# A graph layer on one core: bucket numbers moved to PSUM, and the node layer's own part worked out early

## The chip, the cores and the metric

The kernel runs on one core of a Trainium2 chip. A core has five engines with instruction queues of their own: TensorE (PE in the profile, with its weight loads as PEld), VectorE (DVE), ScalarE (ACT), GpSimd (POOL) and SyncE (SP). They share an on-chip memory, SBUF, of 128 partitions; matmuls write to a second memory, PSUM, of eight banks. Engines wait for each other by semaphores. DMAs move data between the chip's main memory and SBUF; they are issued from the queues of SP, ACT or POOL.

The metric is the device time of one execution in microseconds. Before the change three runs took 2500.06 (the median), 2503.01 and 2492.88 us.

## The reference

The kernel computes one layer of a graph network over 12500 nodes with 64 features and 212500 edges (`src`, `dst`, one weight each). The edges come ordered by `dst`. Cut to what matters:

```python
h = jnp.maximum(_layernorm(x, axis=-1), 0.0)
edge_in = jnp.concatenate([h[row], h[col], dist], axis=1)   # row = src, col = dst
e = silu(edge_in @ eW1 + eb1)
e = silu(e @ eW2 + eb2)
agg = segment_sum(e, row, num_segments=12500)
node_in = jnp.concatenate([h, agg], axis=1)
out = x + silu(node_in @ nW1 + nb1) @ nW2 + nb2
```

The hidden width is 128. `nW1` has 64 rows for the node's own `h` and 128 for the sums `agg`; the product with the first is "the part from a node's own rows".

## The kernel before, in words

The nodes are dealt into `NB` = 100 buckets of `L` = 125 nodes. An edge's bucket is that of its `src`. The kernel first writes the edges, in their given order, into bucket order in main memory (the array `q`), and then works bucket by bucket, so that the sums over `src` become matmuls.

**Tables.** `groups`, `normed` and `products` (L641 to L684) normalise the rows, turn them with PE (`turned`, tile `hr`, two buckets' features one above the other on 128 partitions), store the turned rows in main memory as `hd`, and multiply them by the two halves of `eW1`; the results are stored as the tables `ta` (for `src`) and `tb` (for `dst`). These are generators. They are strung together in `feed`, and each call of `next(feed)` issues one step of them, between other work.

**Sending.** The edges are sent in 208 blocks of 1024. `count(s)` (L344 to L410) ranks the edges of a block within their buckets on VectorE: `oh` (L352) compares the bucket numbers 1 to 100, from a constant row `nodes1` in SBUF, with each edge's bucket; `each` (L360) sums it over the block's 8 columns; PE adds `each` to `full` (L369, L387), a tile of PSUM that keeps the running counts of all buckets; `mine` (L402) multiplies `oh` by `full`, `rank` (L404) sums that, and `to` (L406) is the row number in `q`. `send(s)` (L412 to L467) makes the payload: `qp` (L427, PE) picks the `dst` table's rows, ACT copies it to `qs` (L437, L443), and POOL scatters 128 rows at a time with eight indirect DMAs (L450). There are 4 buffers of `to` and 8 of `qs`, so VectorE and ACT can be some blocks ahead of POOL.

**Buckets.** The rows of `q` are worked on in twelve levels of ranks, each as soon as the blocks that fill it are sent. A step takes four tiles of 128 edges: `lr` (L526) and `oneT` (L531) make the transposed one-hot of the node within the bucket, `pt` (L540, L546) adds the `src` table, ACT applies SiLU to `e` (L550), `p` (L578) is the second layer with its bias copied ahead (L572), SiLU again (L582), `one` (L559) is the one-hot, `seg` (L592) the sum by matmul, and `aggT` (L603) the running sum in SBUF. There are 450 steps.

**Node layer.** In the last level, whose 25 steps hold four buckets each, `nodes` (L239 to L260) follows each step. Two matmuls `z` multiply `aggT` by the lower part of `nW1` (L246), two more add the own rows' part from `hd` (L249), ACT applies SiLU (L251), four matmuls `o` multiply by `nW2` (L255), VectorE adds `x` (L258), and SP stores the result (L260). `nodes_in` (L230) loads `x` and `hd` when the level's rows are fetched, four steps ahead.

**Order.** The order on PE, VectorE, ACT and SP is written out by hand: the list `turn` (L610) names the parts of a step with their offsets in steps, and each `None` in it is a hook. At a hook some pieces of the sending are issued, so many that each level is sent in time (`marks`, L897), then up to two steps of `feed` while it lasts, then one piece of the oldest `nodes`. Each engine runs its queue strictly in that order:

```python
turn = [
    (s_pt, 1), (s_add, -2), (s_one_t, 2), None, (s_bias, 1), (s_p2, 0), (s_one, 0), None, (s_seg, -1), None, (s_lr, 3), None,
]
```

Of the kernel before, what the change touches and what calls it, by code (L numbers as in the profile page):

```python
# [28 lines left out]
F32 = mybir.dt.float32  # L29
# [3 lines left out]
AF = mybir.ActivationFunctionType  # L33
OP = mybir.AluOpType
# [4 lines left out]
P = 128  # L39
L = 125  # L40
# [8 lines left out]
TB = BLK // P  # L49
PAIR = 2 * BLK  # L50
BEYOND = 20
G = 4
# [9 lines left out]
FIRST = 4  # L62
# [11 lines left out]
def tile_gnn(ctx: ExitStack, tc: tile.TileContext, x, src, dst, ew, eW1, eb1, eW2, eb2, nW1, nb1, nW2, nb2, out):  # L74
    nc = tc.nc
    N, D = x.shape
# [3 lines left out]
    NB = N // L  # L80
    assert NB % G == 0 and NB <= P
    NP = -(-E // PAIR)
# [5 lines left out]
    dram = ctx.enter_context(tc.tile_pool(name="dram", bufs=1, space=DRAM))  # L88
# [28 lines left out]
    def rows16(dma, to, of):  # L117

        for part in (slice(0, 112), slice(112, L)):
            dma(to[part], of[part])  # L120
# [21 lines left out]
    nodes1 = const.tile([P, L], F32, name="nodes1")  # L142
    nc.vector.tensor_copy(nodes1, nodes_i)
    w1 = const.tile([P, 2, H], F32, name="w1")
    w1n = const.tile([P, H], F32, name="w1n")
# [61 lines left out]
            nc.scalar.copy(to.rearrange("l (i a) h -> l a i h", a=2)[:, a], abs_[a])  # L207

    hd = dram.tile([P, NB // 2, P], F32, name="hd")
    bkE = const.tile([P, 2 * TB, NP], F32, name="bkE")  # L210
    locE = const.tile([P, 2 * TB, NP], F32, name="locE")
    offE = const.tile([P, 2 * TB, NP], F32, name="offE")
# [17 lines left out]
    def nodes_in(B, sb):  # L230
        b = B * G
        xr = sb.tile([L, G, D], F32, name="xr")
        rows16(nc.sync.dma_start, xr, x_rows[:, b : b + G, :])
        nc.gpsimd.tensor_tensor(xr, xr, nb2b[:L, None, :].to_broadcast([L, G, D]), op=OP.add)
        hr = sb.tile([P, G // 2, P], F32, name="hrn")
        nc.sync.dma_start(hr, hd[:, b // 2 : b // 2 + G // 2, :])
        return xr, hr

    def nodes(B, xr, hr, ps, sb, tag):  # L239

        b = B * G

        zs = sb.tile([P, 2, G // 2, L], F32, name="zs")
        z = [ps.tile([P, G // 2, L], F32, name="z", tag=tag) for _ in range(2)]
        for a in range(2):
            nc.tensor.matmul(z[a], w1g, aggT[:, b + a : b + G : 2, :], start=True, stop=False)  # L246
        for a in range(2):
            half = slice(a * D, (a + 1) * D)
            nc.tensor.matmul(z[a], w1n[half, :], hr[half, :, :L], start=False, stop=True)  # L249
        for a in range(2):  # L250
            nc.scalar.activation(zs[:, a], z[a], AF.Silu, bias=nb1c)  # L251
        yield
        o = ps.tile([L, G, D], F32, name="o", tag=tag)
        for t in range(G):
            nc.tensor.matmul(o[:, t, :], zs[:, t % 2, t // 2, :], w2n, start=True, stop=True)  # L255
        yield
        os_ = sb.tile([L, G, D], F32, name="os")
        nc.vector.tensor_tensor(os_, o, xr, op=OP.add)  # L258
        yield
        rows16(nc.sync.dma_start, out_rows[:, b : b + G, :], os_)  # L260


    NQ = 4
# [5 lines left out]
    with ExitStack() as work:  # L269
# [5 lines left out]
                engines={mybir.EngineType.PE, mybir.EngineType.DVE, mybir.EngineType.Activation, mybir.EngineType.SP}  # L275
            )
        )
        full = sgp.tile([P, NB], F32, name="full")
        nc.tensor.matmul(full, before, identb[:, :NB], start=True, stop=True)
        nc.vector.memset(full, -1.0)  # L280
        mine = cnt.tile([P, TB, NB], F32, name="mine")
        sums = []
        blk, lists = {}, {}
# [60 lines left out]
        def count(s):  # L344

            if s < nblocks:
                bc, win, pick = blk[s]
                p, g = s // 2, s % 2
                whole = p > 0 and (2 * p + 2) * BLK <= E
                buckets = bkE[:, g * TB : (g + 1) * TB, p]  # L350
                oh = wk.tile([P, TB, NB], BF16, name="oh")
                nc.vector.tensor_tensor(  # L352
                    oh,
                    nodes1[:, None, :NB].to_broadcast([P, TB, NB]),
                    buckets[:, :, None].to_broadcast([P, TB, NB]),
                    op=OP.is_equal,
                )
                each = wk.tile([P, NB], BF16, name="each")
                with nc.allow_low_precision("whole numbers up to eight"):
                    nc.vector.tensor_reduce(each, oh.rearrange("p t b -> p b t"), AX.X, OP.add)  # L360
                if not whole:
                    nc.vector.tensor_scalar(pick, bc, same, plus, op0=OP.is_equal, op1=OP.add)
                elif g == 0:
                    nc.vector.tensor_scalar(lists[p][1], lists[p][0], same, plus, op0=OP.is_equal, op1=OP.add)
            yield
            if s < nblocks and (g == 0 or not whole):
                weights(s)
            if s > 0:
                nc.tensor.matmul(full, rest, sums.pop(), start=False, stop=True, skip_group_check=True)  # L369
            limits = [(SURE[w], OP.is_gt) for w in ready_at if s == ready_at[w]]  # L370
            closed = s > 0 and (s == nblocks or needed[s] != needed[s - 1])
            if closed:
                limits.append((SURE[needed[s - 1]], OP.is_lt))
            if s == nblocks:
                limits.append((ROWS, OP.is_gt))
            if limits:
                u = wk.tile([P, NB], F32, name="u")
                v = wk.tile([P, 1], F32, name="v")
            for limit, op in limits:
                nc.vector.tensor_scalar(u, full, float(G * limit - 1), None, op0=op)  # L380
                nc.vector.tensor_reduce(v, u, AX.X, OP.max)
                nc.vector.tensor_tensor(bad[:, 1:2], bad[:, 1:2], v, op=OP.add)
            if s == nblocks:
                return
            if closed and LEVELS[needed[s - 1]][2]:
                nc.vector.tensor_scalar(full, full, float(G * ENDS[needed[s - 1]] - 1), None, op0=OP.max)
            nc.tensor.matmul(full, before, each, start=False, stop=True, skip_group_check=True)  # L387
            sums.append(each)
            if g == 0:
                assert p in scaled  # L390
                both = bkE[:, :, p].rearrange("p (g t) -> p g t", g=2)
                wide = [P, 2, TB, TB]
                eq = wk.tile(wide, F32, name="eq")
                nc.vector.tensor_tensor(
                    eq, both[:, :, :, None].to_broadcast(wide), both[:, :, None, :].to_broadcast(wide), op=OP.is_equal
                )
                nc.vector.tensor_tensor(eq, eq, early[:, None].to_broadcast(wide), op=OP.mult)
                pre = wk.tile([P, 2 * TB], F32, name="pre")
                nc.vector.tensor_reduce(pre.rearrange("p (g t) -> p g t", g=2), eq, AX.X, OP.add)
                nc.vector.tensor_tensor(offE[:, :, p], offE[:, :, p], pre, op=OP.add)  # L400
            yield
            nc.vector.tensor_tensor(mine, oh, full[:, None, :].to_broadcast([P, TB, NB]), op=OP.mult)  # L402
            rank = wk.tile([P, TB], F32, name="rank")
            nc.vector.tensor_reduce(rank, mine, AX.X, OP.add)  # L404
            to = top.tile([P, TB], I32, name="to")
            nc.vector.scalar_tensor_tensor(  # L406
                to, rank, float(G * ROWS - 1), offE[:, g * TB : (g + 1) * TB, p], op0=OP.min, op1=OP.add
            )
            blk[s].append(to)
            yield  # L410
# [353 lines left out]
        def scale(p0, p1):  # L764

            v = bkE[:, :, p0:p1]

            q4 = lp.tile([P, 2 * TB, p1 - p0], F32, name="q4", tag=f"q4{p0}")
            nc.vector.tensor_scalar(q4, v, 0.5 - G / 2 - 1.0, 1.0 / G, op0=OP.add, op1=OP.mult)
            nc.vector.tensor_scalar(q4, q4, float(3 * 2**22), None, op0=OP.add)  # L770
            yield
            nc.vector.tensor_scalar(q4, q4, -float(3 * 2**22), None, op0=OP.add)
            nc.vector.scalar_tensor_tensor(offE[:, :, p0:p1], q4, float(ROWS * G - G), v, op0=OP.mult, op1=OP.add)
            scaled.update(range(p0, p1))
# [36 lines left out]
        with tc.tile_pool(name="lists", bufs=1, side="right") as lp:  # L811
# [54 lines left out]
                    next(feed, None)  # L866
            list(feed)
            windows(1)
            feed = itertools.chain(sources(FIRST, NP), scale(FIRST, NP), checks(), turns(todo, 3))
            for _ in sending:  # L870
                for _ in range(4):
                    next(feed, None)
# [54 lines left out]
        for t in tails:  # L927
            for _ in t:
                pass


    flag_i = const.tile([1, 1], I32, name="flag_i")
# [9 lines left out]
    with tc.If(flag > 0):  # L942
        general_sums(tc, N, E, NB, H, src, dst, ew, ta, tb, aggT, w1d, eb1b, w2, ident, ones, eb2r, part)
        with tc.tile_pool(name="fin", bufs=2) as fin, tc.tile_pool(name="fps", bufs=4, space=PSUM) as fps:
            for B in range(NB // G):
                for _ in nodes(B, *nodes_in(B, fin), fps, fin, "fps"):
                    pass


def general_sums(tc, N, E, NB, H, src, dst, ew, ta, tb, aggT, w1d, eb1b, w2, ident, ones, eb2r, part):  # L950
# [120 lines left out]
```

## Time and profile before

| | |
|---|---|
| median of 3 runs | 2500.06 us |
| the profiled execution | 2495.92 us |
| its span, first to last instruction | 2494.1 us |
| mean granted TensorE clock | 0.915 |
| PE, DVE, ACT, POOL busy | 2056.3, 1936.9, 1088.6, 1740.7 us |
| scatters (L450) | 1661, mean 1.030 us |
| `oh` (L352) | 208, mean 0.984 us |
| matmuls of the own rows' part (L249) | 100 passes, 17.3 us |
| last scatter starts | 2314.1 us |

The page of the profile gives each engine's busy time and, in 40 slices of the span, its busy share in tenths. A row of the list of groups reads: line, engine, operation, tile written <- tiles read, shape, count | busy us, mean ns of one | idle time of the engine just ahead of them and what ended it. In the list of waits a row reads: who waited <- for whom: us in total, times, the longest. In the timeline a row starts with start and time in us. A matmul in 32-bit floats shows as two passes. What lies at the ends of an engine's idle time is inferred from semaphores; "issue" means that nothing in the profile was waited for.

### The profile page before, as it was taken

To read this page: it belongs to the slowest core of one execution; us is meant where nothing else is said; L and a number is where in the kernel's file an instruction comes from. 1 tells how busy PE (TensorE), PEld (TensorE's weight loads), DVE (VectorE), ACT (ScalarE), POOL (GpSimd) and SP (SyncE) were. 2 spreads that over 40 slices of the span, in tenths; PEclk is the share of its full clock that TensorE was granted. 3 is DMA by queue.
4 is the path that set the end of the run, shared out by engine and by line. 5 is a ranking of instruction groups with operands and counts; after the bars stand their busy time and mean duration, and the time that the engine had idled before them with its cause. 6 is when DMAs were issued, how large, how long until landed. Compare 5 with 4: busy or idle time off the path is not lost.

```text
span 2494.1 us, 46291 instructions
## 1 busy us (share of the span) xinstructions
PE 2056.3 (82%) x16191; PEld 1838.5 (74%) x16191; DVE 1936.9 (78%) x3005; ACT 1088.6 (44%) x2403; POOL 1740.7 (70%) x1712
## 2 busy tenths in 40 slices
PE   3663776655588888998889998899999999999997
PEld 2552665555577777887878887788888899999986
DVE  7885677666788887888878888888888899986532
ACT  2451333322244444544444444455455555554442
POOL 4677777777777777777777777777777777762110
PEclk9575888877899998999999999999999999999999
DMA  4563556555667765676645554555555556665652
GB/s 118 182 213 119 168 183 188 179 166 176 194 198 223 222 198 169 219 222 206 202 152 165 164 164 150 165 165 178 166 168 173 179 167 201 216 205 171 194 164 66
DMA packets 237007, 443.85 MB, mean 178 GB/s; under 512 B 49805, under 2 KB 108736, under 8 KB 236562
## 3 DMA queue, kind: packets, MB, share of 16 engines
q1 hardware_dynamic: 158629, 269.79, 35.4%
q0 software_dynamic: 53536, 123.03, 14.2%
q10 hardware_dynamic: 24602, 47.98, 6.6%
q8 instruction: 132, 2.16, 0.4%
q14 instruction: 108, 0.88, 0.1%
HBM read 251.07 MB, written 189.55 MB: 177 GB/s over the span
## 4 chain that ended last, share of the span: by engine, by line
PE 39%; DMA 17%; POOL 14%; DVE 13%; issue 8%; ACT 2%; SPq 0%; DVEq 0%; POOLq 0%; ACTq 0%
DMA q<-qs,to 15%; POOL q L450 14%; PE seg L592 9%; PE pt L546 8%; PE p L578 7%; PE pt L540 4%; PE qp L427 4%; PE lr L526 2%; DVE oh L352 2%; DVE oneT L531 2%; DVE each L360 2%; DVE one L559 2%; DVE aggT L603 2%; DMA qt<-q 1%; DVE mine L402 1%
## 5 line engine op out<-in xcount | busy, mean ns | idle before, releaser
L450 POOL DMA_INDIRECT q<-qs,to x1661 | 1711.6, 1030 | 586.1 <-issue 402.2
L550 ACT ACTIVATE e<-pt 128x512 f32<-128x512 f32 x450 | 268.7, 597 | 867.4 <-PE pt L546 865.2
L592 PE MATMUL seg<-one,e 128*128 128x125 f32 x3600 | 510.3, 287 | 119.0 <-DVE aggT L603 83.7
L592 PEld LDWEIGHTS seg<-one,e 128*128 128x128 f32 x3600 | 462.1, 201 | 170.0 <-issue 110.8
L578 PEld LDWEIGHTS p<-w,e 128*128 128x128 f32 x3600 | 472.0, 196 | 54.2 <-issue 37.3
L546 PE MATMUL pt<-oneT,a 125*128 125x128 f32 (+1 forms) x2400 | 486.8, 337 | 20.0 <-DVE oneT L531 20.0
L578 PE MATMUL p<-w,e 128*128 128x128 f32 x3600 | 494.1, 281 | 0.0
L546 PEld LDWEIGHTS pt<-oneT,a 125*128 125x128 f32 x2400 | 366.3, 199 | 40.6 <-DVE oneT L531 23.1
L437 ACT COPY qs<-qp 128x512 f32<-128x512 f32 x416 | 224.7, 588 | 370.9 <-PE qp L427 321.9
L531 DVE TENSOR_SCALAR oneT<-lr,part 125x512 f32<-125x512 f32 x450 | 335.0, 745 | 48.8 <-PE lr L526 46.8
L360 DVE TENSOR_REDUCE each<-oh 128x100 bf16<-128x800 bf16 x208 | 315.8, 1518 | 7.2
L559 DVE TENSOR_TENSOR one<-nodes,qt 128x500 f32<-128x500 f32 x450 | 302.3, 672 | 0.0
L540 PE MATMUL pt<-ident,qt 128*128 128x128 f32 x1800 | 288.3, 285 | 1.3 <-DVE oneT L531 1.3
L427 PE MATMUL qp<-win,pick 64*128 64x256 f32 x1662 | 270.5, 440 | 22.5 <-DMA win<-tb 6.1
L582 ACT ACTIVATE e<-p 128x512 f32<-128x512 f32 x450 | 268.6, 597 | 27.9 <-PE p L578 27.6
L572 ACT COPY p<-b2f 128x512 f32<-128x512 f32 x450 | 267.2, 594 | 0.0
L406 DVE SCALAR_TENSOR_TENSOR to<-rank,offE 128x8 int32<-128x8 f32 x208 | 36.2, 174 | 280.0 <-DMA q<-qs,to 274.8
L427 PEld LDWEIGHTS qp<-win,pick 64*128 64x128 f32 x1662 | 165.4, 206 | 98.5 <-issue 63.0
L540 PEld LDWEIGHTS pt<-ident,qt 128*128 128x128 f32 x1800 | 201.8, 148 | 48.7 <-issue 38.8
L603 DVE TENSOR_TENSOR aggT<-aggT,seg 128x500 f32<-128x500 f32 x275 | 184.0, 669 | 67.8 <-PE seg L592 64.3
L404 DVE TENSOR_REDUCE rank<-mine 128x8 f32<-128x800 f32 x208 | 205.1, 986 | 7.2
L402 DVE TENSOR_TENSOR mine<-oh,full 128x800 f32<-128x800 bf16 x208 | 203.8, 980 | 6.8 <-PE full L387 6.6
(144 smaller groups left out, 1457.0 us busy)
## 6 DMA issues: line engine op xcount, KB each, us to landing
qt<-q SPq DMA_DIRECT2D x150, 576.0 KB
a<-ta SPq DMA_DIRECT2D x300, 256.0 KB
qt<-q SPq DMA_DIRECT2D x150, 288.0 KB
q<-zeros ACTq DMA_DIRECT2D x25, 1080.0 KB
q<-qs,to POOLq DMA_INDIRECT x1661
q<-zeros ACTq DMA_DIRECT2D x10, 1440.0 KB
bc<-dests SPq DMA_DIRECT2D x103, 128.0 KB
win<-tb SPq DMA_DIRECT2D x416, 30.0 KB
```

The source lines that it names most:

```text
L360: nc.vector.tensor_reduce(each, oh.rearrange("p t b -> p b t"), AX.X, OP.add)
L427: nc.tensor.matmul(qps[i][:, t, : n_of[t]], pick[at, t * P : (t + 1) * P], win[at, : n_of[t]], start=True, stop=True)
L450: ins = nc.gpsimd.indirect_dma_start(out=q[:], out_offset=bass.IndirectOffsetOnAxis(ap=to[:k, j : j + 1], axis=0), in_=qs[:k, t, a, :], in ...
L531: nc.vector.tensor_scalar(oneT, st[k].pop("lr")[:L], part1[:L, :], None, op0=OP.is_equal)
L540: nc.tensor.matmul(pt[:, t, :], qt[:, j, :H], ident, is_transpose=True, start=t == 0, stop=False, skip_group_check=True)
L546: nc.tensor.matmul(pt[:, cols, :], a[:L, b, :], oneT[:, cols, :], start=False, stop=True, skip_group_check=True)
L550: nc.scalar.activation(e1, pt, AF.Silu)
L559: nc.vector.tensor_tensor(one.rearrange("p (b j) l -> p b j l", j=n), nodes1[:, None, None, :].to_broadcast(wide), loc[:, tiles[0][1] : ti ...
L572: nc.scalar.copy(p2, b2f)
L578: nc.tensor.matmul(p2[:, t, :], e1[:, t, :], w2, start=False, stop=t == G - 1, skip_group_check=True)
L582: nc.scalar.activation(e2, p2, AF.Silu)
L592: nc.tensor.matmul(item[2][:, b, :], e2[:, t, :], one[:, t, :], start=j < G, stop=j >= G * (n - 1))
```

## The change

Two things are changed that have nothing to do with each other.

First, the tile `full` of running counts becomes the first half of a tile `counts` of 200 columns in the same bank of PSUM. The second half, `numbers`, receives a copy of the bucket numbers 1 to 100 once, at the start. The comparison `oh` reads `numbers` instead of the row `nodes1` in SBUF; its other input, the edges' buckets, stays in SBUF.

Second, the own rows' part of the node layer becomes a generator `node_part`, one for each four buckets, put at the end of `feed`, two at a time: load `hd`, two matmuls, two copies by ACT to SBUF, a store to a new array `zd` in main memory. `nodes_in` loads `zd` instead of `hd`. In `nodes` the two matmuls of the own rows are gone; at the next hook VectorE adds the loaded part to `z` from PSUM (two instructions), and ACT applies SiLU to both halves in one instruction out of SBUF. The stages of `nodes` after that come one hook later, and the store of the output is handed on (`unsent`) and issued behind the first matmuls of the next `nodes`, or at the end.

```diff
+    zd = dram.tile([P, NB // G, 2, G // 2, L], F32, name="zd")
...
+        zh = sb.tile([P, 2, G // 2, L], F32, name="zh")
+        nc.sync.dma_start(zh, zd[:, B])
+        return xr, zh
+
+    def node_part(B, ps, sb, tag):
+
+        b = B * G
         hr = sb.tile([P, G // 2, P], F32, name="hrn")
         nc.sync.dma_start(hr, hd[:, b // 2 : b // 2 + G // 2, :])
-        return xr, hr
-
-    def nodes(B, xr, hr, ps, sb, tag):
+        yield
+        z = [ps.tile([P, G // 2, L], F32, name="zp", tag=tag) for _ in range(2)]
+        for a in range(2):
+            half = slice(a * D, (a + 1) * D)
+            nc.tensor.matmul(z[a], w1n[half, :], hr[half, :, :L], start=True, stop=True)
+        zh = sb.tile([P, 2, G // 2, L], F32, name="zn")
+        for a in range(2):
+            nc.scalar.copy(zh[:, a], z[a])
+        yield
+        nc.sync.dma_start(zd[:, B], zh)
+        yield
+
+    unsent = []
+
+    def send_out():
+
+        if unsent:
+            rows16(nc.sync.dma_start, *unsent.pop())
+
+    def nodes(B, xr, zh, ps, sb, tag):
...
         for a in range(2):
-            nc.tensor.matmul(z[a], w1g, aggT[:, b + a : b + G : 2, :], start=True, stop=False)
+            nc.tensor.matmul(z[a], w1g, aggT[:, b + a : b + G : 2, :], start=True, stop=True)
+        send_out()
+        yield
         for a in range(2):
-            half = slice(a * D, (a + 1) * D)
-            nc.tensor.matmul(z[a], w1n[half, :], hr[half, :, :L], start=False, stop=True)
-        for a in range(2):
-            nc.scalar.activation(zs[:, a], z[a], AF.Silu, bias=nb1c)
+            nc.vector.tensor_tensor(zs[:, a], z[a], zh[:, a], op=OP.add)
+        nc.scalar.activation(zs, zs, AF.Silu, bias=nb1c)
         yield
...
         nc.vector.tensor_tensor(os_, o, xr, op=OP.add)
-        yield
-        rows16(nc.sync.dma_start, out_rows[:, b : b + G, :], os_)
+        unsent.append((out_rows[:, b : b + G, :], os_))
...
-        full = sgp.tile([P, NB], F32, name="full")
+        counts = sgp.tile([P, 2 * NB], F32, name="counts")
+        full, numbers = counts[:, :NB], counts[:, NB:]
         nc.tensor.matmul(full, before, identb[:, :NB], start=True, stop=True)
         nc.vector.memset(full, -1.0)
+        nc.vector.tensor_copy(numbers, nodes1[:, :NB])
...
                 nc.vector.tensor_tensor(
                     oh,
-                    nodes1[:, None, :NB].to_broadcast([P, TB, NB]),
+                    numbers[:, None, :].to_broadcast([P, TB, NB]),
                     buckets[:, :, None].to_broadcast([P, TB, NB]),
...
-            feed = itertools.chain(sources(FIRST, NP), scale(FIRST, NP), checks(), turns(todo, 3))
+            later = turns([node_part(B, mm, fp, "mm") for B in range(NB // G)], 2)
+            feed = itertools.chain(sources(FIRST, NP), scale(FIRST, NP), checks(), turns(todo, 3), later)
...
         for t in tails:
             for _ in t:
                 pass
+        send_out()
```

## The prediction

> **What bounds the kernel now.** I read the page's totals first, then the waits, then the busy time of single stages, and last the timeline. The page gives the engines, POOL's busy tenths in 40 slices of the span (2494.1 us) and the scatters; two comparisons of VectorE follow from the list of groups (busy time, mean ns of one | idle time before them):
>
> ```profile
> PE 2056.3 (82%) x16191; PEld 1838.5 (74%) x16191; DVE 1936.9 (78%) x3005; ACT 1088.6 (44%) x2403; POOL 1740.7 (70%) x1712
> ...
> POOL 4677777777777777777777777777777777762110
> ...
> L450 POOL DMA_INDIRECT q<-qs,to x1661 | 1711.6, 1030 | 586.1 <-issue 402.2
> ```
>
> ```profile
> L352 DVE TENSOR_TENSOR oh<-nodes,bkE 128x800 bf16<-128x800 f32 x208 | 204.8, 984 | 0.0
> L402 DVE TENSOR_TENSOR mine<-oh,full 128x800 f32<-128x800 bf16 x208 | 203.8, 980 | 6.8 <-PE full L387 6.6
> ```
>
> POOL looks far from full at 70%, but its digit stays at 7 from the third slice to the 35th, and its idle time is "issue": about 0.3 us behind each of 1317 scatters, with nothing to wait for. A scatter of 0.967 us (the median) plus 0.30 us is a beat of 1.27 us, and POOL keeps it from about 135 us to about 2230 us. Who waits for POOL shows that it is the bound. These are two rows of the list of waits, the first over the whole span, the second over 1600 to 2000 us:
>
> ```profile
> DVE to L406 <- DMA q<-qs,to: 274.8, 92, 8.2
> ```
>
> ```profile
> DVE to L406 <- DMA q<-qs,to: 23.4, 13, 3.9
> ```
>
> VectorE has the next block's row numbers (`to`) ready and waits for a buffer that a scatter still reads. By windows these waits are 102.0 us in 300 to 700, 45.3 in 700 to 1100, 61.4 in 1100 to 1600, 23.4 in 1600 to 2000, and none in 2000 to 2200. In the timeline the first scatter of a block starts 25 to 30 us after its `to` was ready, from block 16 to block 192 (2099 us); by block 204 it is 14 us, and its payload (`qs`) is then ready only 5 us ahead, at block 205 0.5 us. So POOL sets the pace until about 2000 us, and the order of work on PE from there on. Two stages (PE, PEld, DVE, ACT and POOL busy; then granted clock, DMA share, GB/s):
>
> ```profile
> 1600.00:2000.00 400.00, 375.79 (x3057) 340.34 (x3056) 348.68 (x527) 204.15 (x436) 308.24 (x302) 0.99 0.53 172
> 2340.00:2464.00 124.00, 124.00 (x1009) 109.22 (x1008) 48.62 (x83) 51.08 (x105) 14.50 (x20) 1.00 0.49 149
> ```
>
> PE is 94% busy in the first (in 2000 to 2200 it is 97%) and 100% in the last, in which the node layer runs.
>
> **Part 1: the comparison reads its bucket numbers from PSUM.** The timeline shows why this can matter to POOL. Here are two stretched scatters and the VectorE instructions about them:
>
> ```profile
> 1541.13 1.43 POOL L450 DMA_INDIRECT q<-qs,to  x1 [0.30 <-issue]
> ```
>
> ```profile
> 1506.47 0.67 DVE L559 TENSOR_TENSOR one<-nodes,qt 128x500 f32<-128x500 f32 x1
> ...
> 1506.66 1.32 POOL L450 DMA_INDIRECT q<-qs,to  x1 [0.30 <-DVE oneT L531]
> 1507.06 0.98 DVE L352 TENSOR_TENSOR oh<-nodes,bkE 128x800 bf16<-128x800 f32 x1
> ```
>
> The scatter at 1506.66 takes 0.35 us too long; `one` ends at 1507.14, which is 0.35 us after 1506.79. The scatter at 1541.13 starts inside an `oh` (1540.74 to 1541.72) and takes 0.46 us too long. I sorted the 1661 scatters of the timeline by the VectorE instruction under way 0.13 us after their start. Under `oh`: 152, 126 of them stretched, 55.2 us together beyond 0.967 each. Under `one` (both inputs in SBUF): 151, 35.0 us. Under `eq`: 68, 7.3 us. Under `mine`, `oneT` and the additions to `aggT`, which read PSUM: 487, 0 us. Under nothing: 291, 0 us. The stretch is what is left of the VectorE instruction. So a two-input instruction with both inputs in SBUF holds a starting scatter up, and one with an input in PSUM does not. After the change `oh` has one of each, as `mine` has.
>
> Of the 55.2 us, what falls while POOL sets the pace counts: 37.0 us in 135 to 1600 (15.5, 10.0 and 11.5 in three windows) and 12.6 us in 1600 to 2000, where VectorE has 23.4 us of waiting to give up. The 2.1 us before 135 (POOL waits for its first blocks) and the 3.4 us from 2000 on (PE at 97%) are counted as nothing. The remaining 35 us under `one` grow with the density of `one`, 2.3% or 1 us. I take 49.6 - 1 = **48 us less**. Ends: 55 us less if all counts; 0 if what matters is that the second operand is in SBUF, since beside scatters no row has its first operand in PSUM and its second in SBUF (`mine` and `aggT` have it the other way round). I take 48, as every row with one PSUM input says 0 stretch.
>
> The Trainium skill, "SBUF — State Buffer", section "SBUF: two separate sides", says that VectorE with two SBUF inputs and GpSimd contend for one port pair, that whoever starts first keeps it for its whole instruction, and that the other blocks. The trace agrees for a scatter that comes second; for an `oh` that comes second it would make records of up to 1.9 us, while the longest `oh` is 1.05 us against a median of 0.983, so the measurement decides that VectorE has nothing to win here.
>
> What `oh` itself costs from PSUM: `mine`, of the same 800 columns and with a PSUM input, 0.980 us against 0.984, so 0. The dearest row of 800 columns is the strided reduction `each`, 1.518 us; at that price 208 x 0.53 = 111 us on VectorE, covered by its 274.8 us of waiting up to about 1600 us and not later (39 blocks in 1600 to 2000 have 23.4 us: at worst 12.6 + 39 x 0.53 - 23.4 = 10 us of the gain would go, and 16 blocks x 0.53 = 8 us after 2000). The set-up copy of 100 columns is one instruction of about 0.26 us (row `u`) in the start.
>
> The Trainium skill, "VectorE: DVE Perf Modes", section on the errata, speaks against this edit: it gives 58 + columns cycles from SBUF and 120 + columns from PSUM. By it `oh` would be 62 cycles or 65 ns dearer, 13 us of VectorE in all, still inside its waiting; the two rows show no such difference.
>
> **Part 2: the node layer.** At the end one step (4 buckets) takes 5.89 us of full PE, 2431.97 to 2437.86. PE's matmuls in it (start, time; `lr` follows):
>
> ```profile
> 2431.97 0.61 PE L540 MATMUL pt<-ident,qt 128*128 128x128 f32 x4
> 2432.42 1.06 PE L546 MATMUL pt<-oneT,a 125*128 125x128 f32 x8
> 2433.31 1.01 PE L246 MATMUL z<-aggT,w1g 128*128 128x250 f32 x4
> 2434.25 0.69 PE L249 MATMUL z<-hrn,w1n 64*128 64x250 f32 x4
> 2434.88 1.16 PE L578 MATMUL p<-w,e 128*128 128x128 f32 x8
> 2435.87 0.98 PE L255 MATMUL o<-w2n,zs 128*125 128x64 f32 x8
> 2436.69 1.11 PE L592 MATMUL seg<-one,e 128*128 128x125 f32 x8
> ```
>
> Start to start, L249 takes 0.63 us. Without it a step would be 5.26 us: 25 x 0.63 = 15.7 us less. But the order changes: the addition and the SiLU are issued one hook later, so ACT has them behind `e<-p`, and PE has `o` behind `seg`. Counted from the start of `p`: ACT's `e<-p` can start at 1.25 (2470.70 against 2469.45 in the last steps, where nothing else holds it). The next ACT instruction follows 0.51 later, at 1.76. SiLU of 500 columns out of SBUF, from 0.429 for 256 and 0.848 for 768 (rows of L626), is 0.63: it ends at 2.39, and `o` starts at 2.44. PE is through with `p` (0.99) and `seg` (0.95) at 1.94 and waits 0.50. The step becomes 5.26 + 0.50 = 5.76, 0.13 less. VectorE is not later: the two additions (0.42 each, as `os`) end at about 0.7, and `os`, then `aggT`, end about 1.2 ahead of `p`, 0.25 before `z` needs them. 22 steps x 0.13 = 3 us; the last three, which have no other PE work, lose about 0.4 each, 1 us. **4 us less.** Ends: 15.7 less (no wait for `o`) and 5 more (0.2 a step dearer, if the hop between engines is that much longer). The output's DMAs go out one hook later on SP and hold up only loads four steps ahead.
>
> The part from the own rows moves into the feed: 25 loads and 25 stores on SP, 50 matmuls, 50 ACT copies (0.377 as `hr`, 19 us). In the order of PE all of it lies between the last products (200 us) and the first `seg`. In 200 to 300 us PE is 49% and ACT 27% busy, POOL has 28 us of work in hand, and the matmuls are 16 us. I take **0**. Upper end 11 us, from the rival below; no gain is possible there. The tail loads 256 KB instead of 128 a step, at a DMA share of 0.49: 0.
>
> Sum: 2495.92 (the profiled execution; 2494.1 span and 1.8 around it) - 48 - 4 = 2443.9. The median of the runs shown is 4.1 above that execution, so I say **2448 us**.
>
> **The rivals.**
> A: the second operand holds the port wherever the first lies. For it: no counterexample of that form. Against: `aggT`'s and `mine`'s 0 us. Then only the 4 us remain: 2496, no change that can be measured.
> B, slower: the new rounds in the feed hold PE up. Two batches go round together: two loads (0.34 issue each), landing up to 2.8 (`qt`, 243.42 to 246.25), two times 4 passes (0.69 at full clock, 1.05 at the 0.66 of that stage), 0.8 of copies, 0.8 of stores, after which alone the next loads are issued: 7.2 us. 12.5 rounds are 90 us, against 51 us of idle PE and 28 us of POOL's stock: 11 us lost, 2459. It decides from 10.5 us a round, where 131 us - 79 eat the 52 us gained; at 12 us a round 2519.
> C: PE takes over early. It idles 14% in 700 to 1200 but 6% in 1600 to 2000. If half the stretch turns into waits elsewhere, 25 us remain: 2475.
>
> **How the numbers follow.** My forecast, 2426 to 2472, 0.77; C 0.08; A 0.11; B to the point of slower 0.04. The low end is the full 55 us and most of the 15.7 (2500 - 55 - 15.7 is 2429); the high end is C with the node step 5 us dearer, 2480. A measurement of this kernel tells 0.5% (12.5 us) from no change. Faster holds forecast and C, 0.85; same is A, 0.11; slower B, 0.04.
>
> **What the profile after would show.** The scatter's mean falls from 1030 to about 997 ns, with stretches under `one` left; `oh` stays at 0.98; blocks follow each other in 10.25 us instead of 10.5; POOL's last scatter comes near 2265 instead of 2314; the last steps take about 5.75 us with a wait of `o` for ACT. A mean still at 1030 would say A. POOL waiting for `qs` between 200 and 400 us would say B. Waits of VectorE for scatters gone before 1600 would say C.

## The result and the profile after

The changed kernel takes 2467.41 us (median; 2461.50 to 2471.29), the kernel before 2499.50 us measured beside it (2492.88 to 2503.01): a ratio of 0.9873, 95% interval 0.9844 to 0.9901. It is 1.3% faster, 32 us where 52 were forecast. The profiled execution took 2466.53 us, 29.4 less than that of before.

The page of the changed kernel, its totals, POOL's busy tenths in 40 slices, and three groups (busy time, mean ns of one | idle time before them); the lines of the source have moved, L450, L402 and L352 are now L476, L428 and L378:

```profile
span 2464.8 us, 46494 instructions
...
PE 2057.6 (83%) x16191; PEld 1842.7 (75%) x16191; DVE 1953.1 (79%) x3056; ACT 1100.1 (45%) x2428; POOL 1703.8 (69%) x1712
...
POOL 4677677777777777777777777777777777762110
...
L476 POOL DMA_INDIRECT q<-qs,to x1661 | 1674.7, 1008 | 595.8 <-issue 400.0
...
L428 DVE TENSOR_TENSOR mine<-oh,counts 128x800 f32<-128x800 bf16 x208 | 204.0, 981 | 29.3 <-PE counts L413 29.2
...
L378 DVE TENSOR_TENSOR oh<-counts,bkE 128x800 bf16<-128x800 f32 x208 | 204.4, 983 | 0.0
```

The scatter's mean fell from 1030 to 1008 ns, 36.9 us over 1661 scatters, not to the 997 forecast. `oh` costs the same (983 ns, 984 before). POOL's digits have one new dent, a 6 in the fifth slice (246 to 308 us). Two rows of the list of waits over the whole span tell of the pace and of the shared tile (total, times, longest):

```profile
DVE to L432 <- DMA q<-qs,to: 202.6, 79, 6.5
...
PE counts L395 <- DVE oh L378: 61.4, 17, 7.8
```

VectorE still waits for scatters, 202.6 us where it was 274.8, and 83.3, 35.1, 54.9 and 21.8 us of it lie in the windows 300 to 700, 700 to 1100, 1100 to 1600 and 1600 to 2000. So POOL still sets the pace. The second row is new and comes from the shared tile: the matmul `rest` writes the counts and `oh` reads the numbers in one tile, so the one waits for the other. It takes the place of a part of PE's waiting for `each` (141.4 us before, 44.8 after); what it costs is seen below from the pace with both comparisons in that tile. A tile of its own in PSUM for the numbers was not tried.

Sorted as in the prediction (by the VectorE instruction under way 0.13 us after a scatter's start; count, and stretch beyond 0.967 us). Where the records of two instructions overlap at that moment, a comparison (`oh`, `one`, `eq`) goes before any other; if the one that started last were taken, `one` would have 150 before and 200 after, with 34.9 and 53.6 us:

```
           under oh          under one         under eq
before     152   55.2 us     151   35.0 us     68   7.3 us
after      135    0.3 us     221   54.3 us     53   5.4 us
```

And by time: the first scatter of a block, with its lead, which is the time since VectorE started the instruction that writes its row numbers (`to`):

```
block            16            24            32            64     128     192            last scatter   span
before   222.1 (30.0)  305.1 (28.3)  389.9 (25.9)  729.8  1416.9  2098.6 (28.0)  2314.1         2494.1
after    217.0 (28.6)  306.7 (10.0)  391.7 (24.1)  722.9  1397.6  2072.1 (28.0)  2286.9         2464.8
```

The gain of 5 us at block 16 is gone at block 24, where the lead of 28 us has shrunk to 10; from block 32 on the kernel gains steadily, 27.2 us at the last scatter, and another 2.1 after it.

### The profile page after: what moved, and what is told of

The parts are those of the page before. It is cut to its first block, busy times and chain, and to the rows that moved or that the text cites. A ratio compares the mean times of both kernels' runs of the same rounds, so it can differ in the third digit from the quotient of the medians.

```text
span 2464.8 us, 46494 instructions
## 1 busy us (share of the span) xinstructions
PE 2057.6 (83%) x16191; PEld 1842.7 (75%) x16191; DVE 1953.1 (79%) x3056; ACT 1100.1 (45%) x2428; POOL 1703.8 (69%) x1712
## 4 chain that ended last, share of the span: by engine, by line
PE 39%; DMA 17%; DVE 15%; POOL 11%; issue 8%; ACT 3%; SPq 1%; DVEq 0%; POOLq 0%; ACTq 0%
DMA q<-qs,to 14%; POOL q L476 11%; PE pt L572 8%; PE seg L618 8%; PE p L604 7%; PE qp L453 5%; PE pt L566 4%; PE lr L552 2%; DVE oneT L557 2%; DVE oh L378 2%; DVE each L386 2%; DVE one L585 2%; DVE aggT L629 2%; DMA hrn<-hd 1%; DVE mine L428 1%
## 5 line engine op out<-in xcount | busy, mean ns | idle before, releaser
L476 POOL DMA_INDIRECT q<-qs,to x1661 | 1674.7, 1008 | 595.8 <-issue 400.0
L618 PE MATMUL seg<-one,e 128*128 128x125 f32 x3600 | 502.6, 285 | 99.6 <-DVE aggT L629 76.9
L618 PEld LDWEIGHTS seg<-one,e 128*128 128x128 f32 x3600 | 455.5, 199 | 129.5 <-issue 64.0
L604 PEld LDWEIGHTS p<-w,e 128*128 128x128 f32 x3600 | 475.9, 197 | 29.7 <-issue 11.3
L428 DVE TENSOR_TENSOR mine<-oh,counts 128x800 f32<-128x800 bf16 x208 | 204.0, 981 | 29.3 <-PE counts L413 29.2
L378 DVE TENSOR_TENSOR oh<-counts,bkE 128x800 bf16<-128x800 f32 x208 | 204.4, 983 | 0.0
```

The source lines that it names most:

```text
L476: ins = nc.gpsimd.indirect_dma_start(out=q[:], out_offset=bass.IndirectOffsetOnAxis(ap=to[:k, j : j + 1], axis=0), in_=qs[:k, t, a, :], in ...
L604: nc.tensor.matmul(p2[:, t, :], e1[:, t, :], w2, start=False, stop=t == G - 1, skip_group_check=True)
L618: nc.tensor.matmul(item[2][:, b, :], e2[:, t, :], one[:, t, :], start=j < G, stop=j >= G * (n - 1))
```

## The experiments

Each kernel computes everything. Those of the first group are compared with a median of 2496.12 us of the kernel before, those of the second with 2494.49 us. This is what their traces gave, by the same sorting; "tail" is the time from the start of the last scatter to the end of the span:

```
               under oh     under one    mean ns  block 24 (lead)  last scatter  tail
before         152  55.2    151  35.0    1030     305.1 (28.3)     2314.1        180.0
after          135   0.3    221  54.3    1008     306.7 (10.0)     2286.9        177.9
part 1 alone   136   0.2    211  57.6    1012     300.9 (29.7)     2285.2        180.5
part 2 alone   136  50.2    149  35.3    1031     309.1 (10.0)     2317.0        176.8
one too        162   0.0    186   0.0     976     305.4 (9.4)      2246.4        176.3
paced feed     137   0.2    216  54.8    1009     300.6 (28.0)     2279.4        178.2
SiLU earlier   126   0.1    214  52.4    1010     307.5 (10.0)     2288.5        161.8
one, not oh    161  51.1    148  -0.1    1005     308.1 (9.4)      2287.8        177.7
all three      165   0.0    197  -0.1     977     301.1 (28.8)     2241.8        161.3
no part 2      152  -0.1    209   0.0     977     299.7 (27.6)     2239.3        179.8
```

**Part 1 alone**, with the node layer of before:

```diff
-        full = sgp.tile([P, NB], F32, name="full")
+        counts = sgp.tile([P, 2 * NB], F32, name="counts")
+        full, numbers = counts[:, :NB], counts[:, NB:]
...
+        nc.vector.tensor_copy(numbers, nodes1[:, :NB])
...
-                    nodes1[:, None, :NB].to_broadcast([P, TB, NB]),
+                    numbers[:, None, :].to_broadcast([P, TB, NB]),
```

> Part 1 alone: the bucket numbers lie in PSUM, the node layer is that of before. Theory: the gain of the change comes from scatters no longer held by oh, and the change lost some 7 us of it between 217 and 307 us, where the new loads of hd let POOL run dry. Then this kernel keeps those 7 us: stretch under oh near 0, under one near 54 us, the first scatter of block 24 starts over 20 us after its to was ready (10 us in the changed kernel), a step of the last level at 5.89 us, and a time of about 2466 us (2460 to 2470), as fast as the whole change. Rival: the feed cost nothing and the missing part of the gain is all in the stretch that moved to one; then block 24 is at the place of the changed kernel, and the time is that of the changed kernel plus the 3 us of the last level, 2470 or more.

Measured: 2467.49 us, ratio 0.9880 (0.9861 to 0.9900): the whole gain of the change, within its interval. The wait for the shared tile is here too, and larger, with no loss to be seen beside it:

```profile
DVE to L408 <- DMA q<-qs,to: 246.0, 90, 7.0
...
PE counts L371 <- DVE oh L354: 86.0, 24, 7.3
```

`oh` lost its stretch, and `one` took up 22.6 us of it with no node layer in the feed: part 2 is not what raised `one`. Block 24 starts 5.8 us earlier than in the changed kernel, with its lead of 29.7 us, but the last scatter only 1.7: by their mean (1012 against 1008 ns) the scatters here are stretched by 5.8 us more.

**Part 2 alone**, the changed kernel with the comparison as before:

```diff
-        counts = sgp.tile([P, 2 * NB], F32, name="counts")
-        full, numbers = counts[:, :NB], counts[:, NB:]
+        full = sgp.tile([P, NB], F32, name="full")
...
-                    numbers[:, None, :].to_broadcast([P, TB, NB]),
+                    nodes1[:, None, :NB].to_broadcast([P, TB, NB]),
```

> Part 2 alone: oh reads its bucket numbers from SBUF as before, the node layer is the changed one. Theory: a step of the last level takes 5.68 us instead of 5.89 and the tail wins 3 us, the feed loses up to 7 us between 217 and 307 us because POOL runs dry: 2499 to 2505 us, stretch under oh near 55 us and under one near 35 us, as before. Rival: the feed is hidden; then 2496 us and block 24 starts when it did before (305 us).

Measured: 2501.37 us, ratio 1.0025 (1.0010 to 1.0039). The last scatter is 2.9 us later, the tail 3.2 shorter, and nothing is won. The list of waits names the loads of the feed:

```profile
PE zp L249 <- DMA hrn<-hd: 48.5, 13, 7.7
```

**`one` too from PSUM**, in the changed kernel:

```diff
-        counts = sgp.tile([P, 2 * NB], F32, name="counts")
+        counts = sgp.tile([P, NB + L], F32, name="counts")
...
-        nc.vector.tensor_copy(numbers, nodes1[:, :NB])
+        nc.vector.tensor_copy(numbers, nodes1)
...
-                    numbers[:, None, :].to_broadcast([P, TB, NB]),
+                    numbers[:, None, :NB].to_broadcast([P, TB, NB]),
...
-                nodes1[:, None, None, :].to_broadcast(wide),
+                numbers[:, None, None, :].to_broadcast(wide),
```

> The changed kernel, and one (the one-hot of the nodes) reads its 125 numbers from PSUM too, from the same tile. Theory: a VectorE instruction with two inputs in SBUF is what holds a starting scatter, so the 54 us under one go as well; blocks follow in 10.2 us; VectorE still waits 195 us for scatters between 300 and 2000 us in the changed kernel, so some 40 us arrive at the end: about 2427 us (2418 to 2440). Rival: PE or VectorE takes over, or the shared tile makes one wait for PE: the waits of VectorE for scatters go away before 1600 us, and the time stays above 2452 us.

Measured: 2424.74 us, ratio 0.9717 (0.9697 to 0.9738). From its page and its list of waits:

```profile
L476 POOL DMA_INDIRECT q<-qs,to x1661 | 1621.2, 976 | 608.1 <-issue 398.5
...
L585 DVE TENSOR_TENSOR one<-counts,qt 128x500 f32<-128x500 f32 x450 | 301.1, 669 | 5.3 <-PE counts L413 4.6
```

```profile
DVE to L432 <- DMA q<-qs,to: 145.8, 54, 6.5
...
PE counts L395 <- DVE one L585: 73.8, 56, 7.9
```

The 54.3 us under `one` are gone, the scatter is down to 976 ns, and 42.1 us of span go with them. `one` costs 669 ns, 672 from SBUF. PE now waits for `one` because of the shared tile, and it is not what holds the end: a block follows the other in 10.23 us (387.0 at block 32, 1942.2 at block 184), which is eight beats of 1.27 and little else.

**The feed spread out.** Each `yield` of `node_part` becomes six, so its loads, matmuls and stores come a sixth as often:

```diff
-        yield
+        for _ in range(6):
+            yield
```

> The changed kernel, with six yields in place of each in node_part: the same loads, matmuls, copies and stores are issued at a sixth of the pace, most of them behind the first step of the buckets. Theory: POOL ran dry because the loads of hd came round faster than they land, with PE waiting for each; at this pace it does not: the first scatter of block 24 is again over 20 us behind its to, and the time is 7 us shorter, about 2460 us (2455 to 2464). Rival: the work itself costs, not its haste; then the loss moves to 300 to 700 us and the time stays at 2467 us.

Measured: 2459.58 us, ratio 0.9860 (0.9837 to 0.9883). The matmuls of the own rows lie between 203.7 and 663.1 us instead of 198.4 and 294.8, block 24 keeps its lead, and POOL no longer runs dry. The last scatter is 7.5 us earlier than in the changed kernel. The intervals of the two ratios overlap (0.9873 there), so it is the traces that tell the two apart. The last experiment below gives the same size without any stretch in the way.

**The addition and the SiLU one hook earlier**, right behind `z`, so that ACT has them ahead of `e<-p`:

```diff
         send_out()
-        yield
         for a in range(2):
             nc.vector.tensor_tensor(zs[:, a], z[a], zh[:, a], op=OP.add)
         nc.scalar.activation(zs, zs, AF.Silu, bias=nb1c)
         yield
+        yield
```

> The changed kernel, with the addition and the SiLU of the node layer issued at the hook of the z matmuls (one hook earlier); o and all behind it stay where the change put them. Theory: a step of the last level takes 5.68 us instead of about 5.2 because PE waits for o, whose SiLU stands behind e<-p on ACT; here it stands ahead of it, the wait goes, and 22 steps of 0.45 us or 10 us are won: about 2457 us (2454 to 2461). Rival: something else holds the step, the additions that now stand ahead of one on VectorE or the later os and aggT; then a step stays above 5.5 us and the time above 2463 us.

Measured: 2452.16 us, ratio 0.9829 (0.9806 to 0.9852), with the tail 16.1 us shorter than in the changed kernel. Here is PE's timeline in a step of the tail (start, time), and ACT's in the same step:

```profile
2388.36 1.01 PE L271 MATMUL z<-aggT,w1g 128*128 128x250 f32 x4
2389.22 1.05 PE L604 MATMUL p<-w,e 128*128 128x128 f32 x8
2390.11 1.05 PE L618 MATMUL seg<-one,e 128*128 128x125 f32 x8
2390.99 0.99 PE L280 MATMUL o<-w2n,zs 128*125 128x64 f32 x8
2391.82 0.39 PE L552 MATMUL lr<-identb,qt 128*125 128x128 bf16 x4
```

```profile
2389.87 0.71 ACT L275 ACTIVATE zs<-zs,nb1c 128x500 f32<-128x500 f32 x1 [0.71 <-DVE zs L274]
2390.49 0.58 ACT L598 COPY p<-b2f 128x512 f32<-128x512 f32 x1
2391.00 0.58 ACT L608 ACTIVATE e<-p 128x512 f32<-128x512 f32 x1
```

The SiLU is done at 2390.58, before PE is through with `seg`, and `o` starts without a wait. The next step's `z` starts at 2393.39: a step takes 5.03 us.

**`one` from PSUM, `oh` from SBUF**, the kernel of the third experiment with one line of it undone:

```diff
-                    numbers[:, None, :NB].to_broadcast([P, TB, NB]),
+                    nodes1[:, None, :NB].to_broadcast([P, TB, NB]),
```

> The changed kernel with the two comparisons exchanged: one reads its numbers from PSUM, oh from SBUF again. The change took away 55 us of stretch under oh and got 19 us back under one. Theory: the two follow each other closely on VectorE, and a scatter that the one no longer holds is caught by the other more often; so here stretch under one is 0 and that under oh rises from 55 to some 75 us, and the time is about 2483 us (35 won, 20 given back, 7 lost in the feed, 3 won at the end). Rival: the rise under one had nothing to do with oh; then stretch under oh stays within 50 to 60 us, and the time is about 2466 us.

Measured: 2471.15 us, ratio 0.9903 (0.9887 to 0.9919).

```profile
L476 POOL DMA_INDIRECT q<-qs,to x1661 | 1670.1, 1005 | 601.3 <-issue 404.0
...
L585 DVE TENSOR_TENSOR one<-counts,qt 128x500 f32<-128x500 f32 x450 | 300.7, 668 | 4.7 <-PE counts L413 4.3
...
L378 DVE TENSOR_TENSOR oh<-nodes,bkE 128x800 bf16<-128x800 f32 x208 | 204.2, 982 | 0.0
```

The theory of an exchange in both directions fell: `oh` holds 51.1 us, no more than before. What it does show is that `one` is caught 148 times while `oh` holds scatters, whether or not `one` itself holds them.

**All three together**: both comparisons from PSUM, the feed spread out, the SiLU earlier; its diff is the sum of the three above.

> All three together: one and oh read their numbers from PSUM, node_part at a sixth of the pace, and the node layer's addition and SiLU one hook earlier. Theory: from 2425 us with the first alone, 7 us less for the pace and 10 us less at the end: about 2408 us (2403 to 2415). Rival: PE sets the pace well before 2000 us in the first already, and what POOL wins early is lost again: only the 10 us of the end arrive, 2414 us or more.

Measured: 2403.09 us, ratio 0.9627 (0.9610 to 0.9645), faster than both kernels. The two rows of its windows 1600 to 2000 and 2000 to 2200 (PE, PEld, DVE, ACT, POOL busy; clock, DMA share, GB/s), and a wait in the second of them:

```profile
1600.00:2000.00 400.00, 389.59 (x3247) 356.16 (x3246) 365.37 (x557) 214.74 (x459) 304.57 (x314) 1.00 0.55 179
2000.00:2200.00 200.00, 192.99 (x1784) 184.31 (x1783) 175.49 (x272) 100.71 (x209) 123.29 (x128) 1.00 0.65 201
```

```profile
POOL q L479 <- ACT qs L472: 29.8, 8, 14.6
```

Here PE is 97% busy in both windows. Until about 2000 us POOL has little to spare either: a block follows the other in 10.23 us (383.0 at block 32, 1938.0 at block 184). From 2110 us POOL waits for payloads, and what is left to win there lies with PE.

**Both comparisons from PSUM with the node layer of before**: part 1 alone, and the line of `one`.

> one and oh read their numbers from PSUM, and the node layer is that of the kernel before, without any of the second edit. Theory: it lacks the 7 us that the feed lost and the 3 us that the end won: about 2421 us (2416 to 2426), so the second edit as it was made is a loss of some 4 us, and is worth some 13 us only with the slower pace and the earlier SiLU. Rival: the own rows' matmuls, 16 us of PE, matter more where PE sets the pace: 2428 us or more.

Measured: 2422.59 us, ratio 0.9710 (0.9692 to 0.9727). With part 2 as made it is 0.9717, with part 2 spread out and its SiLU earlier 0.9627. So with POOL freed, the second part as made is worth nothing that can be measured, and made the other way 19.5 us. Its two halves can be read from the table: with `one` too from PSUM and part 2 as made, the last scatter starts 7.1 us later than here, and the tail is 3.5 us shorter.

## Why the prediction was right, and where its sizes were off

The forecast was 2448 us in 2426 to 2480; it became 2467.41. Its sign and its cause hold, two large terms of its sum do not. That the time still lies within the range is in part luck: the upper end, 2480, was worked out from rival C and a dearer node step, neither of which came, and it had room for two misses that were not foreseen.

**"After the change `oh` has one of each, as `mine` has": right.** 55.2 us became 0.3, and rival A, that the second operand holds the port wherever the first lies, is refuted by 135 scatters. The Trainium skill, "SBUF — State Buffer", section "Who interferes with whom", says that a VectorE instruction with at most one SBUF input, outside certain fast modes, does not contend with GpSimd; the 0.3 us under `oh` and the 0.0 under `one` agree with it.

**"What `oh` itself costs from PSUM": right, 0** (983 ns against 984). The Trainium skill, "VectorE: DVE Perf Modes", section on the errata, has 62 cycles more for a source in PSUM, by estimate 65 ns; they do not show in `oh`, nor in `one` (669 against 672 ns), which have one of their two inputs there.

**"The remaining 35 us under `one` grow with the density of `one`, 2.3% or 1 us": the step that failed.** These 35 us grew by 19.3 us, in part 1 alone by 22.6, and so the blocks follow each other in 10.49 us (391.7 at block 32, 1986.8 at block 184) where 10.25 was foretold. The pace before was 10.68 (389.9 at block 32, 2013.0 at block 184), not the 10.5 of the prediction, so that 0.19 us a block was won instead of 0.25. The 151 scatters of before were taken as a rate, and they were a product of the very holds that were to go. A rate can be worked out without them: from 135 us on, 420 `one` of 0.672 us pass while the changed kernel's scatters start every 1.35 us, which makes 209 starts inside a `one`. In the seven kernels in which `oh` holds nothing the count is 186 to 221; in the three in which it holds, 148 to 151 (181 to 200 against 147 to 150 if the instruction that started last is taken). The working from the rows of before would have been the same 420 x 0.672 / 1.364 = 207, and with the mean stretch of 35.0 / 151 it gives 48 us, 13 us more than before; the measured stretch per scatter is slightly larger, 0.246 us. For `oh` that count gives 197 x 0.984 / 1.364 = 142 where 152 were seen.

How the holds of `oh` spare `one` is told by their timing, which fits but is not a proof. A held scatter ends 0.84 us behind the instruction that held it and the next starts 0.30 later, so that one starts 1.14 us behind the end of `oh`, whatever came before, and of 114 such next scatters none started under `oh` or `one`: they fell within `each`, 1.52 us long, which follows `oh`. VectorE's order repeats, and a `one` that began 4 to 6 us after an `oh` caught a scatter in 15 of 67 cases before and 21 of 77 in the kernel with `one` alone in PSUM, but in 43 of 71 after the change. That reads as if the holds had lined POOL up with VectorE.

**"I take 0" for the feed, upper end 11 us from rival B: the second step that failed.** The mechanism that B described came in part. The own rows' matmuls took 96.4 us for 12.5 rounds, 7.7 a round (B worked out 7.2). PE waited 49.8 us for their loads; two of these waits, and what they did to POOL, in the timelines of PE and POOL:

```profile
245.02 2.04 PE L249 MATMUL zp<-hrn,w1n 64*128 64x250 f32 x8 [3.61 <-DMA hrn<-hd]
256.17 1.21 PE L249 MATMUL zp<-hrn,w1n 64*128 64x250 f32 x4 [9.11 <-DMA hrn<-hd]
```

```profile
284.85 0.96 POOL L476 DMA_INDIRECT q<-qs,to  x1 [2.02 <-ACT qs L469]
...
288.65 0.97 POOL L476 DMA_INDIRECT q<-qs,to  x1 [0.30 <-issue]
295.90 0.97 POOL L476 DMA_INDIRECT q<-qs,to  x1 [6.28 <-ACT zn L252]
```

That is the sign named for B, POOL waiting for `qs` between 200 and 400 us. (The last row names `zn`, a copy that was under way on ACT; the copy to `qs` just ahead of it ended at 295.63, 0.27 us before the scatter.) POOL used up its lead and ran dry for 7.7 us beyond its usual gap. Those 7.7 us are what the paced feed gave back (7.5 at the last scatter). The 28 us of lead and the idle time of PE were counted as cover in full; the loads stop PE in its order of work, and the idle time of PE was not where the waits fell.

**The node layer's step: right in its order, small in its size.** Predicted 5.76 us with a wait of `o` for ACT of 0.50; here is one step of the tail, PE and ACT:

```profile
2402.37 1.01 PE L271 MATMUL z<-aggT,w1g 128*128 128x250 f32 x4
...
2403.22 1.05 PE L604 MATMUL p<-w,e 128*128 128x128 f32 x8
...
2404.11 1.05 PE L618 MATMUL seg<-one,e 128*128 128x125 f32 x8
2404.31 0.60 ACT L608 ACTIVATE e<-p 128x512 f32<-128x512 f32 x1 [0.65 <-PE p L604]
2404.80 0.70 ACT L276 ACTIVATE zs<-zs,nb1c 128x500 f32<-128x500 f32 x1
...
2405.56 1.09 PE L280 MATMUL o<-w2n,zs 128*125 128x64 f32 x8 [0.40 <-ACT zs L276]
```

The SiLU stands behind `e<-p`, as worked out, and `o` waits 0.40 for it; the step is 5.68 us (`o` to `o`, 2399.88 to 2405.56). The part of it that was off is "without it a step would be 5.26 us": it is 5.03 with the wait gone. Start to start, `z` takes 0.85 instead of 0.94 and `p` 0.89 instead of 0.99.

**"The last three ... lose about 0.4 each" was wrong, but by less than this trace alone says.** They were to become shorter. From the start of the fourth last `o` to that of the last matmul it took 17.43 us before and 19.30 after. Most of the difference lies in one step of 7.31 us, in which the granted clock was 0.76 (2434 to 2441 us) and `z` took 1.99 us instead of 1.08:

```profile
2436.14 1.99 PE L271 MATMUL z<-aggT,w1g 128*128 128x250 f32 x4 [1.25 <-DVE aggT L629]
```

With part 2 alone and with `one` too the clock was 1.00 in that step; it took 5.65 us, and the whole stretch 17.63 and 17.66. So without the low clock the last three became 0.2 us longer together, not 1 us shorter: `z` waits 1.25 us for `aggT` in them, where it was 0.77 before. The paced feed has the low clock in the same step too (0.76, and 7.21 us); what lowered it is not shown. On the other side 22 steps at 0.21 are 4.6 us less. The tail as a whole won 2.1 us in this execution, and 3.2 and 3.7 in the two where the clock held: near the 4 foretold, but only because two misses cancel. Part 2 by itself, "4 us less" with the feed at 0, still came out 0.25% slower (5 us by the medians).

The sum: 55 us less under `oh`, 19 more under `one`, 8 more for the feed and 2 less in the tail make 30 less, against 29.3 of the span. It closes to a few us and no better: it lets all 55 us count where the prediction let 49.6, and the scatters became 36.9 us shorter, the feed took 7.7 of it, and of the 29.2 left 27.2 had arrived at the last scatter. Rival C, PE taking over early, did not come before 2000 us: VectorE kept its waits for scatters in all four windows (and PE's idle time in 700 to 1200 before was 13%, 64.0 of 500 us, not 14%).

## What to carry to other kernels

Beside indirect DMAs that POOL issues back to back, give each two-input VectorE instruction one operand in PSUM, and do it to all of them together: here one comparison alone, `oh` or `one`, was worth 1.3% or 1.0%, both 2.8%, each with part 2 as made. Holds of one instruction can shield the next, so count what will be hit by share of time, not by what the trace shows now. Work put into an in-order feed with a DMA round trip inside wants spreading, since its waits eat the lead of whoever comes behind. When a stage moves one hook on, look which instruction the next engine now runs first; here one hook was worth 16 us of the tail.

## What was not expected of the hardware

Putting the same constant in PSUM for a second instruction brought another 42 us at no cost in either instruction: it is the cheapest edit in this study. The shielding works in one direction alone: without the holds of `oh`, `one` was hit 186 to 221 times instead of about 150, but without those of `one` the stretch under `oh` stayed at 51.1 us. And the matmuls of 64 rows were worth more than their own slot: without them and with `o` behind `seg` the step fell by 0.86 us (5.89 to 5.03), not by the 0.63 of that slot, since `z`, `p` and `seg` became shorter by 0.08, 0.10 and 0.07, start to start. Whether the missing matmuls or the new order of the others shortens them was not tried.
